# Loading x tile by tile and the value weights in four pieces in a hybrid convolution and attention kernel

## The chip, the cores and the metric

The kernel runs on one core of one Trainium2 chip, in one launch. The metric is the device time of that launch in microseconds (us); before the change its median over three runs is 1225.91 us.

## The reference

The input x has 4 images of 16 x 16 pixels with 1024 channels: 1024 tokens in all. Everything is float32. Cut to what matters:

```python
# layer 0: lambda convolution over the group-normalised x
x = x + L0_conv(_gn(x), Wq, Wk, Wv, q_*, v_*, rel_pos_emb)   # q, softmax(k), v; Yc + Yp
# layer 1: causal attention and a mixture of 8 experts
t = _to_tokens(x)
t = t + L1_attn(_ln_t(t), W_attn, b_attn, W_proj, b_proj)
t = t + L1_ffn(_ln_t(t), gate_w, gate_b, expert_w, expert_b)

def L1_attn(x, W_attn, b_attn, W_proj, b_proj):
    qkv = jnp.einsum('btc,oc->bto', x, W_attn) + b_attn
    q, k, v = jnp.split(qkv, 3, axis=2)          # 16 heads of 64
    ...                                          # masked softmax, weighted sum of v
    return jnp.einsum('btc,oc->bto', y, W_proj) + b_proj

def _ln_t(v, eps=1e-5):
    m = jnp.mean(v, axis=-1, keepdims=True)
    s = jnp.var(v, axis=-1, keepdims=True)
    return (v - m) / jnp.sqrt(s + eps)
```

The change lies where the output of layer 0 is added to x and the result is normalised for the attention (the first `_ln_t`, "layer norm 1"), and where the weights of the value projection, the last third of `W_attn`, are fetched.

## The kernel before

The kernel is one long function for one core. Layer 0 comes first (group norm, its projections, position terms), then layer norm 1 with the residual sum of layer 0, then the attention's value products, its query and key products with the softmax, the output projection, and the experts. Many products of matrices are done in Strassen's manner, with seven products of halves in place of eight, which is why sums of blocks (`sums_of_A`, L159) stand beside them.

**The stretch of the change** begins at L574. `x_at` holds all of x as eight tiles of 128 tokens (512 KB each); `xs[t]` is tile t. It takes the place of `xn`, the normalised input of layer 0, so its loads have to wait until the last product that reads `xn` (`v_product`, L538) is done. `tiles` is the order in which the tiles are worked on: the four tiles of the second halves of the images, then the four of the first halves. L578 to L580 issue all eight loads on POOL's queue, one after the other, and then the load of the bias `bp` (L589), which is 512 KB in SBUF too.

**The loop of layer norm 1** (L622 to L641) makes one pass i for each of the first seven tiles; the eighth follows behind it (L642). The order of every engine is as written here (`manual_schedule`, L621). In one pass:

- `spread(i)` (L591): `content` (L446) of the next tile, L452 on PE into PSUM and L460 on DVE, which adds it into `s0`; then the products `py` (L603) of this tile on PE, and two additions of them to `xs[t]` on DVE (L610). `s0` is filled from `two_T` by many small moves on SP's queue (L487), which were issued before.
- `layer_norm` (L192): statistics on DVE (L197 to L199), the root on ACT, and one ACTIVATE that writes the normalised rows to a slice of `ln_rows` (L170, three slices in turn; for the last two tiles L206).
- `turn_quarters(i - 2)` (L613): DVE's transpose (L187) of the tile of two passes ago into `ln1`, from its `quarters`.
- for the first six tiles, `turn_by_rows` (L210): SP writes the rows to DRAM (L212), and when they have landed reads them back in four pieces into `quarters` (`quarters_of`, L182). The last two tiles are transposed on PE instead (`turn_on_pe`, L219, with ACT's copies L223).
- in pass 3 only, L637 issues the load of `w_v[0]` on SP behind the tile's reads: the first half of the value weights, 8 blocks of 128 rows by 512 columns, as one DMA of 2 MB (`w_tile`, L123; the DMA is at L129).
- for the first six tiles, POOL adds `bp` to `xs[t]` (L638), and stores it to `x_rows` in DRAM (L639), from where the output projection takes it much later. The last two tiles are stored by SP (L641, L643).

`ln_rows`, `w_v[0]` and earlier `w_kv` come from `wpool`, a pool with two buffers: `w_v[0]` takes the buffer of `w_kv`, whose last reader is `v_product`, and `w_v[1]` (L738) takes the one of `ln_rows`.

Behind the loop, in written order too: POOL's sums of the blocks of `w_v[0]` (`sums_v`, L718), and on PE the first value products (`first`, L682, at L665) of tiles 1 and 3, the transposes of the seventh tile, the products of tile 0, the transposes of the eighth tile, and the products of tile 2. Then the load of `w_v[1]` and the other products of the first half follow. From L755 on a planner orders the instructions by its own costs until the next written order (L941): the second half of the values and the query and key products of the first pair of heads.

Of the kernel before, what the change touches and what calls it, by code (L numbers as in the profile page):

```python
# [32 lines left out]
F32 = mybir.dt.float32  # L33
# [6 lines left out]
P = 128  # L40
C = 1024
NC = C // P
# [3 lines left out]
NT = TOK // P  # L46
# [11 lines left out]
HALF = 512  # L58
# [11 lines left out]
def kernel(  # L70
# [27 lines left out]
    nc = tc.nc  # L98

    def pool(stack, name, bufs=1, **kw):  # L100
        return stack.enter_context(tc.tile_pool(name=name, bufs=bufs, reuse_waits="tile", **kw))
# [16 lines left out]
    wpool = pool(right, "wpool", 2, side="right")  # L118
# [4 lines left out]
    def w_tile(name, *parts, home=None, queue=nc.sync):  # L123

        w = (home or wpool).tile([P, NC, HALF], F32, tag="w", name=name)
        at = 0
        for part in parts:
            n = part.shape[1]
            queue.dma_start(w[:, :, at : at + n], part.rearrange("(c p) n -> p c n", p=P))  # L129
            at += n  # L130
        return w
# [60 lines left out]
    def layer_norm(ln, t, on_pe=False):  # L192


        stats = small.tile([P, 2, 6], F32, tag="ln_stats", name=f"ln1_stats{t}")
        for j in range(2):
            nc.vector.bn_stats(stats[:, j, :], xs[t][:, ts(j, HALF)])  # L197
        mv = small.tile([P, 2], F32, tag="ln_mv", name=f"ln1_mv{t}")
        nc.vector.bn_aggr(mv, stats)  # L199
        rstd = small.tile([P, 1], F32, tag="ln_rstd", name=f"ln1_rstd{t}")  # L200
        inverse_root(rstd, mv[:, 1:2], EPS)
        if on_pe:
            less = small.tile([P, 1], F32, tag="ln_less", name=f"ln1_less{t}")
            nc.vector.scalar_tensor_tensor(less, mv[:, 0:1], -1.0, rstd, ALU.mult, ALU.mult)
            for j in range(2):
                nc.scalar.activation(ln[:, ts(j, HALF)], xs[t][:, ts(j, HALF)], AF.Identity, bias=less, scale=rstd)  # L206
            return
        normalised(ln, xs[t], mv[:, 0:1], rstd)

    def turn_by_rows(ln, t, quarters, turns):  # L210
        rows = turns.tile([P, Q, C // Q], F32, tag="rows", name=f"ln1_rows{t}")
        nc.sync.dma_start(rows.rearrange("n f c -> n (f c)"), ln)  # L212
        quarters_of(rows, quarters)
# [13 lines left out]
    with ExitStack() as layer0:  # L227
# [16 lines left out]
        with ExitStack() as projection:  # L244
# [96 lines left out]
            with tc.manual_schedule():  # L341
# [6 lines left out]
                for c in range(NC):  # L348
# [10 lines left out]
                    elif NC - 4 < c < NC - 1:  # L359
                        n = c - (NC - 3)  # L360
# [26 lines left out]
            for n in (1, 2, 3, 5, 4, 7, 6):  # L387
                for pair, ((a11, a12, a21, a22), (c11, c12, c21, c22), (s1, s2, s3, s4)) in enumerate(pairs):
                    a, b = {
                        1: (a11, b11),  # L390
                        2: (a12, b21),
                        3: (s4, b22),
                        5: (s1, b11),
                        4: (a22, b21),
                        7: (s3, b12),
                        6: (s2, b22),
                    }[n]
# [28 lines left out]
            for t in range(NT):  # L426
                b, kc = divmod(t, 2)
# [147 lines left out]
        xs = [x_at[:, t, :] for t in range(NT)]  # L575
        late = pool(x_home, "late", 2, side="right")
        tiles = [(b, nt) for nt in (1, 0) for b in range(B)]
        for b, nt in tiles:  # L578
            t = 2 * b + nt
            nc.gpsimd.dma_start(xs[t], x[ts(t, P), :])  # L580

# [7 lines left out]
        def spread(i):  # L591
            b, nt = tiles[i]
            t = 2 * b + nt
            if i == 0:
                content(b, nt)
            if i + 1 < NT:
                content(*tiles[i + 1])
            for hp in range(2):
                py = mm(f"py{t}_{hp}")
                for hl in range(2):  # L600
                    bh = b * HEADS0 + 2 * hp + hl
                    for mh in range(2):
                        nc.tensor.matmul(  # L603
                            py[:, ts(hl, M)],
                            s0[:, mh, ts(nt, S2), :, bh].rearrange("p i j -> p (i j)"),
                            v_T[:, mh, ts(b, M)],
                            start=(mh == 0),
                            stop=(mh == 1),
                        )
                nc.vector.tensor_add(xs[t][:, ts(hp, HALF)], xs[t][:, ts(hp, HALF)], py)  # L610
            return t

        def turn_quarters(i):  # L613
            of, quarters = to_turn[i]
            turn(ln1[:, :, ts(of, P)], quarters)
# [2 lines left out]
            of[:, :C].rearrange("p (f c) -> p f c", f=Q)  # L618
            for of in (emb.rearrange("p c i j -> p (c i j)"), s_w.rearrange("p a c n -> p (a c n)"))
        ]  # L620
        in_order.enter_context(tc.manual_schedule())  # L621
        for i in range(NT - 1):  # L622
            t = spread(i)
            quarters = None
            if i < NT - 2:
                if i < NT - 4:
                    quarters = spare[i % 2]
                else:
                    quarters = late.tile([P, Q, C // Q], F32, tag="xg", name=f"ln1_quarters{t}")
            to_turn.append((t, quarters))  # L630
            layer_norm(ln_rows[:, i % 3, :], t, i >= NT - 2)
            if i >= 2:
                turn_quarters(i - 2)
            if i < NT - 2:
                turn_by_rows(ln_rows[:, i % 3, :], t, quarters, turns)
                if i == 3:
                    w_v = [w_tile("w_v0", W_attnT[:, 2 * C : 2 * C + HALF])]  # L637
                nc.gpsimd.tensor_add(xs[t], xs[t], bp)  # L638
                nc.gpsimd.dma_start(x_rows[ts(t, P), :], xs[t])  # L639
            else:  # L640
                nc.sync.dma_start(x_rows[ts(t, P), :], xs[t])  # L641
        t = spread(NT - 1)  # L642
# [4 lines left out]
    with ExitStack() as attention:  # L647
# [293 lines left out]
        with tc.manual_schedule():  # L941
            for d in range(len(doubles) + lag):
# [24 lines left out]
                if d < 14:  # L967
# [6 lines left out]
                    if d == 13:  # L974
                        sums.close()
                        x_pool = pool(x_home, "xb", side="right")
                        xs = [x_pool.tile([P, C], F32, tag=f"x{t}", name=f"xb{t}") for t in range(NT)]
# [120 lines left out]
    with ExitStack() as gating:  # L1098
# [350 lines left out]
        w, bias, step, T, T3, A, S = {0: w0}, {0: bias0[0]}, {}, {}, {}, {}, {}  # L1449
# [235 lines left out]
    with tc.If(count > SLOTS), ExitStack() as rest:  # L1685
        w_rest, l3 = pool(rest, "w_rest", 4), pool(rest, "l3", 3)
        for e in range(E):
            w_e = [half_weights(e, r, w_rest, "w_r") for r in range(2)]
            tiles = range(SLOTS // P, NT - 1 if e in SHORT else NT)
# [60 lines left out]
```

## Time and profile before

| what | us |
|---|---|
| median of three runs | 1225.91 |
| lowest and highest run | 1224.85 and 1229.62 |
| profiled execution, its own time | 1227.45 |
| its span (first to last instruction) | 1225.6 |
| PE busy in the span | 1208.7 |
| loads of x issued on POOL (L580) | 207.3 to 210.9 |
| additions of layer 0's output (L610) | 215.4 to 272.5 |
| load of `w_v[0]`: issue and time to landing | 252.4, 11.7 |
| first value product (L665) | 264.1 |

Times of events are counted from the start of the span. PE is the engine of the matrix products, PEld its weight loads, DVE, ACT and POOL the engines for vectors, activations and general work, and SP the engine whose queue issues most transfers. A line of the order in time has the start, the duration from first to last, the engine, the line of the kernel, the operation, what it writes and reads, the number of instructions, and in brackets how long its engine was idle before the first of them, and for whom. A line of the waits has the waiting engine and line, the one waited for, the total in us, how many times, and the longest. A line of stretches has the stretch, its length, the busy time and number of instructions of PE, PEld, DVE, ACT and POOL, the granted clock of PE, the busy share of the 16 DMA engines and the GB/s that they moved.

### The profile page before, as it was taken

How to read it: one execution, taken by the hardware profiler on the slowest of the kernel's cores; microseconds unless marked ns; L12 is line 12 of the kernel's file. 1: busy time of each engine (PE TensorE's matmuls, PEld its weight loads, DVE VectorE, ACT ScalarE, POOL GpSimd, SP SyncE). 2: the span in 40 equal slices, each digit the busy share in tenths (PEclk: the TensorE clock that was granted, in tenths of full speed). 3: DMA queues.
4: the chain of work that ended last, by engine and by line, in shares of the span. 5: the costliest groups of instructions: out<-in, count | busy, mean ns of one | idle time of the engine just before them, and what ended most of it. 6: DMA issues, size and time to landing. Idle time of an engine off the chain costs nothing.

```text
span 1225.6 us, 13283 instructions
## 1 busy us (share of the span) xinstructions
PE 1208.7 (99%) x4780; PEld 632.8 (52%) x4780; DVE 721.4 (59%) x1274; ACT 203.8 (17%) x502; POOL 401.5 (33%) x467
## 2 busy tenths in 40 slices
PE   9999999999999999999999999999999999999998
PEld 5444884778884444444444444444344334434443
DVE  5796636668332666565644567666566655565742
ACT  3310111111001222121311212101111111111110
POOL 1051351364000122222232116427443635363521
PEclk9999999999999999999999999999999999999999
DMA  9102014772201353525465646564855576556432
GB/s 349 27 1 69 18 44 123 248 251 94 69 9 60 104 172 104 170 95 181 147 213 192 206 172 238 143 185 95 246 158 141 109 230 182 144 138 180 98 82 55
DMA packets 94121, 169.77 MB, mean 139 GB/s; under 512 B 11968, under 2 KB 48848, under 8 KB 94048
## 3 DMA queue, kind: packets, MB, share of 16 engines
q1 hardware_dynamic: 73600, 108.49, 26.8%
q0 software_dynamic: 16144, 51.45, 17.3%
q10 hardware_dynamic: 4304, 8.91, 2.1%
q8 instruction: 40, 0.66, 0.2%
q14 instruction: 33, 0.27, 0.1%
HBM read 116.12 MB, written 48.50 MB: 134 GB/s over the span
## 4 chain that ended last, share of the span: by engine, by line
PE 87%; DMA 7%; DVE 3%; SPq 2%; issue 1%; ACT 1%; POOL 0%; DVEq 0%; POOLq 0%; ACTq 0%
PE p L1516 31%; PE pqk L665 15%; PE pv L665 7%; PE po L920 5%; PE pq_pair L400 4%; PE left L1558 3%; PE pq L319 3%; PE pT L510 3%; DMA ln_rows<-ln_rows 2%; PE pk L431 2%; PE sc L824 2%; PE pa L893 2%; PE rest L1572 2%; PE pv L538 2%; DMA quarters<-rows 1%; DMA s<-two_T 1%
## 5 line engine op out<-in xcount | busy, mean ns | idle before, releaser
L1041 POOL DMA_INDIRECT w_e_xg<-rows,gather x146 | 156.3, 1071 | 50.9 <-issue 41.4
L1516 PE MATMUL p<-w_e,A 128*128 128x512 f32 x368 | 163.2, 593 | 1.3 <-DVE slot L1328 1.3
L865 POOL TENSOR_TENSOR s_q<-s_q,total 128x128 f32<-128x128 f32 (+1 forms) x128 | 60.2, 506 | 276.5 <-DVE total L862 276.5
L920 PE MATMUL po<-w_p,y_T 128*128 128x512 f32 x256 | 116.8, 607 | 0.0
L1516 PEld LDWEIGHTS p<-w_e,A 128*128 128x128 f32 x368 | 69.6, 190 | 89.9 <-issue 89.0
L1064 POOL DMA_INDIRECT out_dram<-y,add x32 | 56.5, 1766 | 177.5 <-ACT y L1522 114.3
L1516 PE MATMUL p<-T,S 128*128 128x512 f32 x256 | 112.7, 593 | 0.0
L1522 ACT ACTIVATE y<-y,slot 128x512 f32<-128x512 f32 x64 | 46.2, 723 | 333.1 <-DVE y L1530 177.9
L665 PE MATMUL pqk<-ln,w_qk 128*128 128x512 f32 x192 | 85.7, 595 | 0.0
L1516 PEld LDWEIGHTS p<-T,S 128*128 128x128 f32 x256 | 48.6, 190 | 60.8 <-issue 60.5
L850 ACT ACTIVATE s_q<-sc,top 128x128 f32<-128x128 f32 (+1 forms) x128 | 52.1, 420 | 164.4 <-DVE top L846 140.6
L920 PEld LDWEIGHTS po<-w_p,y_T 128*128 128x128 f32 x256 | 47.6, 192 | 54.5 <-issue 53.5
L187 DVE STREAM_TRANSPOSE A<-w_e_xg 128x1024 f32<-128x1024 f32 x32 | 39.7, 1240 | 47.2 <-DMA w_e_xg<-rows,gather 47.2
L665 PEld LDWEIGHTS pqk<-ln,w_qk 128*128 128x128 f32 x192 | 36.1, 190 | 43.7 <-issue 41.9
L665 PE MATMUL pqk<-T,S_qk 128*128 128x512 f32 x128 | 57.8, 595 | 0.0
L1516 PE MATMUL p<-T,A 128*128 128x512 f32 x128 | 57.5, 592 | 0.0
L1516 PE MATMUL p<-w_e,S 128*128 128x512 f32 x128 | 57.5, 592 | 0.0
L665 PE MATMUL pv<-w_v,ln 128*128 128x256 f32 x192 | 43.7, 380 | 1.5 <-ACT ln L223 1.1
L319 PE MATMUL pq<-w_q,xn 128*128 128x512 f32 x96 | 44.5, 599 | 0.3 <-ACT xn L299 0.3
L1558 PE MATMUL left<-w_e,one 128*32 128x512 f32 x312 | 41.8, 593 | 0.0
L1516 PEld LDWEIGHTS p<-w_e,S 128*128 128x128 f32 x128 | 24.3, 190 | 30.6 <-issue 30.1
L1516 PEld LDWEIGHTS p<-T,A 128*128 128x128 f32 x128 | 24.3, 190 | 30.6 <-issue 30.1
(329 smaller groups left out, 1846.5 us busy)
## 6 DMA issues: line engine op xcount, KB each, us to landing
w_e<-in_expert_w_dram SPq DMA_DIRECT2D x12, 2048.0 KB, 15.2
s_rows<-s_q SPq DMA_DIRECT2D x32, 384.0 KB, 2.3
s_rows<-s_rows SPq DMA_DIRECT2D x128, 96.0 KB, 2.3
w_qk<-in_W_attnT_dram SPq DMA_DIRECT2D x8, 1024.0 KB, 5.4
w_e<-in_expert_w_dram ACTq DMA_DIRECT2D x4, 2048.0 KB, 9.5
xn<-in_xT_dram SPq DMA_DIRECT2D x8, 512.0 KB, 7.2
w_q<-in_Wq_dram SPq DMA_DIRECT2D x16, 256.0 KB, 7.3
x_at<-in_x_dram POOLq DMA_DIRECT2D x8, 512.0 KB
```

The source lines that it names most:

```text
L187: nc.vector.transpose(row_T[:, :, :slots].rearrange("p c (g j) -> p g c j", j=32), row[:, : slots // 32, :].rearrange("p g (c i) -> p g c ...
L319: nc.tensor.matmul(pq, xn[:, c, ts(t, P)], w_q[kc][:, c, :], start=(c == 0), stop=(c == NC - 1))
L400: nc.tensor.matmul(bank, a[:, c, :], b[:, c, :], start=(c == 0), stop=(c == NC // 2 - 1))
L665: nc.tensor.matmul(bank, stationary(c), moving(c), start=(c == 0), stop=(c == NC // 2 - 1))
L850: nc.scalar.activation(blocks(h, qt), psc[:, h, cols].rearrange("p (b f i) -> p b f i", f=Q, i=32), AF.Exp, bias=top[:, qt, h : h + 1], sc ...
L865: nc.gpsimd.tensor_mul(blocks(h, qt), blocks(h, qt), total[:, qt, h : h + 1].unsqueeze(2).unsqueeze(3).to_broadcast([P, 1 + qt, Q, 32]),)
L920: nc.tensor.matmul(po, y_T[:, c, ts(t, P)], w_p[j][:, c, :], start=(c == 0), stop=(c == NC - 1))
L1041: nc.gpsimd.indirect_dma_start(out=row[:, g, :], out_offset=None, in_=table[: (TOK - P) * Q, :] if e in SHORT else table, in_offset=bass.I ...
L1064: nc.gpsimd.indirect_dma_start(out=out[: TOK - P, :] if e in SHORT else out, out_offset=bass.IndirectOffsetOnAxis(ap=add[:slots, e, k : k ...
L1516: nc.tensor.matmul(bank, a[:, c, :], b[:, c, :], start=(c == 0), stop=(c == NC // 2 - 1))
L1522: nc.scalar.mul(y[i][:, ts(j, HALF)], y[i][:, ts(j, HALF)], slot[:, e, 1, 2 * pair + i : 2 * pair + i + 1])
L1558: nc.tensor.matmul(bank[ts(i, 32), :], stationary, w[of][j][:, c, :], start=(c == 0), stop=(c == NC - 1))
```

## The change

The eight loads of x are no longer issued together. A helper `load_x1(i)` issues the load of the i-th tile in the order of `tiles`; it is called for the first three tiles where all eight were, and then once in each of the passes 0 to 5, for the tile three passes ahead, on POOL's queue in front of that pass's addition of `bp`. (In pass 5 no tile is left to load.)

The tile `w_v[0]` is allocated ahead of the loop. Its load is split by rows into four DMAs of 512 KB (two blocks of 128 rows each), which are issued on SP's queue in the passes 0, 1, 2 and 3, each behind the reads of that pass's rows.

```diff
-        for b, nt in tiles:
-            t = 2 * b + nt
-            nc.gpsimd.dma_start(xs[t], x[ts(t, P), :])
+
+        def load_x1(i):
+            if i < NT:
+                b, nt = tiles[i]
+                nc.gpsimd.dma_start(xs[2 * b + nt], x[ts(2 * b + nt, P), :])
+
+        for i in range(3):
+            load_x1(i)
...
+        w_v = [wpool.tile([P, NC, HALF], F32, tag="w", name="w_v0")]
         in_order.enter_context(tc.manual_schedule())
         for i in range(NT - 1):
             t = spread(i)
...
             if i < NT - 2:
                 turn_by_rows(ln_rows[:, i % 3, :], t, quarters, turns)
-                if i == 3:
-                    w_v = [w_tile("w_v0", W_attnT[:, 2 * C : 2 * C + HALF])]
+                if i < 4:
+                    some = slice(2 * i, 2 * i + 2)
+                    nc.sync.dma_start(
+                        w_v[0][:, some, :],
+                        W_attnT[2 * i * P : (2 * i + 2) * P, 2 * C : 2 * C + HALF].rearrange("(c p) n -> p c n", p=P),
+                    )
+                load_x1(i + 3)
                 nc.gpsimd.tensor_add(xs[t], xs[t], bp)
                 nc.gpsimd.dma_start(x_rows[ts(t, P), :], xs[t])
```

## The prediction

> **What bounds the kernel now.** I read the page first, then who waited for whom on PE between 206 and 300 us (the stretch that the diff touches), then SP's queue and DVE in order of time there.
>
> ```profile
> span 1225.6 us, 13283 instructions
> ...
> PE 1208.7 (99%) x4780; PEld 632.8 (52%) x4780; DVE 721.4 (59%) x1274; ACT 203.8 (17%) x502; POOL 401.5 (33%) x467
> ```
>
> PE is idle for 1225.6 - 1208.7 = 16.9 us in the whole run. No change of loads can win more; what counts is how much of it lies here.
>
> ```profile
> PE pv L665 <- ACT ln L223: 1.1, 1, 1.1
> PE pc L452 <- DVE s L460: 0.9, 1, 0.9
> PE ln_pt L219 <- ACT ln_rows L206: 0.5, 1, 0.5
> PE pv L665 <- DMA w_v<-in_W_attnT_dram: 0.4, 1, 0.4
> ```
>
> PE's waits here are 2.9 us in all: the ceiling of a gain. Otherwise it runs one tile of layer norm 1 after another, 3.6 us of content products (L452) and 3.7 us of py (L603) overlapping a little: a period of 7.0 us (pc starts at 246.01 and 252.99).
>
> Behind the waits is SP, which takes each normalised tile i (i counts the loop's passes) through DRAM: a write (L212), a wait until it has landed, four reads (L182), then the next write.
>
> ```profile
> 225.22 2.05 SPq L487 DMA_DIRECT2D s<-two_T  x3
> 227.37 0.53 SPq L212 DMA_DIRECT2D ln_rows<-ln_rows  x1
> 232.37 1.97 SPq L182 DMA_DIRECT2D emb<-ln_rows  x4
> 234.44 0.38 SPq L212 DMA_DIRECT2D ln_rows<-ln_rows  x1
> 238.17 2.15 SPq L182 DMA_DIRECT2D s_w<-ln_rows  x4
> 240.42 0.41 SPq L212 DMA_DIRECT2D ln_rows<-ln_rows  x1
> 244.98 1.73 SPq L182 DMA_DIRECT2D emb<-ln_rows  x4
> 246.81 0.38 SPq L212 DMA_DIRECT2D ln_rows<-ln_rows  x1
> 250.42 1.87 SPq L182 DMA_DIRECT2D s_w<-ln_rows  x4
> 252.39 0.40 SPq L129 DMA_DIRECT2D w_v<-in_W_attnT_dram  x1
> 252.89 0.52 SPq L212 DMA_DIRECT2D ln_rows<-ln_rows  x1
> 265.80 2.29 SPq L182 DMA_DIRECT2D ln_quarters<-ln_rows  x4
> ```
>
> The reader is to see three things. The first write is issued at 227.37, though its tile was ready at 221.4 (ACT's L170 starts at 220.13 and takes 1.24): the moves of L487 stand in front. A cycle from write to write then takes 6.0 to 6.4 us, less than PE's 7.0, so SP catches up. And the write behind the 2 MB of w_v needs 12.9 us (252.89 to 265.80) instead of 3.6 to 4.6. DVE shows who pays:
>
> ```profile
> 237.06 1.25 DVE L187 STREAM_TRANSPOSE ln<-emb 128x1024 f32<-128x1024 f32 x1 [3.05 <-DMA emb<-ln_rows]
> 244.04 1.25 DVE L187 STREAM_TRANSPOSE ln<-s_w 128x1024 f32<-128x1024 f32 x1 [1.11 <-DMA s_w<-ln_rows]
> ...
> 270.71 1.25 DVE L187 STREAM_TRANSPOSE ln<-ln_quarters 128x1024 f32<-128x1024 f32 x1 [7.64 <-DMA ln_quarters<-ln_rows]
> ```
>
> The late first turn costs DVE 3.05 us and PE 0.91 at 238.93 (some 2.1 us of DVE delay are absorbed by banks). The turn behind w_v holds the last tile's L610 until 271.88, and with it the ACT steps for which PE waits 0.54 and 1.06 us.
>
> **x loads.** All eight stay on POOL, 0.53 us of issue each. Three go out at 207; x3, in pass 0, stands before the first L638, so right behind bp; x4 to x7 follow in passes 1 to 4, each behind the x_rows store of the pass before: about 224.7, 231.7, 238.6 and 246. They are first read by L610 at 246.38, 252.26, 258.49 and 271.88 now, so even 2.5 us earlier each has over 12 us to land. POOL idles 3.0 to 5.8 us ahead of each L638, which waits for ACT: the moved issues cost nothing. Without that idle time it would be 0.53 us per pass, on a chain that ends in the x_rows store only.
>
> What is gained: between 207 and 224 the loads fill the DMA.
>
> ```profile
> DMA packets 2403, 5.16 MB, mean 304 GB/s; under 512 B 433, under 2 KB 1379, under 8 KB 2403
> ...
> SPq L487 <- DMA s<-two_T: 4.7, 7, 1.1
> ```
>
> 2 of 4.2 MB leave this stretch. The second line, of SP's waits from 204 to 228, is what SP lost to slow landings; I take half as saved, 2.3 us (bounds 0 and 4.7, since the first four tiles still collide). SP's first write moves from 227.4 to about 225.
>
> **Weight pieces.** One DMA of 2 MB becomes four of 512 KB, each behind the reads of passes 0 to 3; three more issues are 3 x 0.39 = 1.2 us on SP, spread over four cycles. A piece stands in SP's queue ahead of the next pass's write, which the next reads wait for, for which DVE waits two passes later, and PE behind DVE. So its price is a longer cycle. The trace has 2 MB in front of one write: 12.9 - 3.6 = 9.3 us, 2.3 per piece, but with two x_rows stores beside it, and start-up. An x tile's 128 packets of 4 KB took about 160 ns on one of 16 engines, 1.3 us in all; I take 1.4 for a piece (bounds 1.3 and 2.3). The x tile that now comes beside it is another 1.3 us of DMA time, on POOL's queue: the stores there lengthen cycles by 0 to 0.4, so I take 0.3 (bounds 0 and 1.3). The cycle becomes 6.2 + 1.4 + 0.3 = 7.9 us (bounds 7.5 and 9.8) for passes 1 to 4, against PE's 7.0. Whole-stretch traffic allows it:
>
> ```profile
> 227.40:252.40 25.00, 24.09 (x87) 18.29 (x86) 17.59 (x36) 5.29 (x7) 9.82 (x7) 1.00 0.64 219
> 252.40:264.40 12.00, 11.58 (x45) 9.42 (x45) 8.69 (x19) 2.89 (x5) 4.76 (x4) 1.00 0.96 323
> ```
>
> DMA is busy for 0.64 (last column but one) of the 25 us; four tiles and four pieces add 4 x 1.3 + 4 x 1.4 = 10.8 us to 16.0: 26.8 over some 30 us, nearly full. That is the weak point of the change.
>
> [...] no one waits for a single piece; in the trace eight loads of 512 KB leave POOL within 4.2 us and move back to back. I take the trace's value[...].
>
> **The sum.** First write 225; the second a cycle of 6.7 later, 231.7 (piece 0 comes behind the reads, so it delays only the write after); write n then at 231.7 + 7.9 (n-1), n = 4 at 255.4. Quarters are turned about 2.2 us after the next write's issue: turns 0 to 3 can go at 233.9, 241.8, 249.7, 257.6. DVE reaches them at 234.0, 241.0, 248.4 and 256.3; lateness of 0.8 to 1.3 us per pass, a third of it reaching PE. What follows turn 3 in DVE is turn 1.25 and L460 1.25, then PE's last py 3.7, in sum (with a handover of 0.1) 6.3: the first pv starts at 263.9 (now 264.08). No wait for w_v: piece 3, issued near 255, lands by 260. Turn 4 can go at 265.5, five us earlier than 270.71, so the last tile is normalised while PE does its 32 pv (7.0) and 8 transposes (1.04), 16 pv (3.7), 8 transposes (1.36) and a rest of 0.3 for L223's copy: 13.4. The pv that starts at 278.75 now starts at 263.9 + 13.4 = 277.3: **1.45 us won**. All behind it shifts along: w_v1's load is released by the same transposes, POOL's sums of w_v by the last py. The profiled execution took 1227.45 for its span of 1225.6; minus 1.5 this is 1226.0. It lies 1.5 above the median 1225.91, 0.1%; so the forecast is 1225.9 - 1.5 = **1224.4 us**.
>
> **Rivals.**
>
> *SP keeps up* (cycle near 7, first write at 223 to 224): turn 3 is ready before DVE, PE only loses the 0.3: 2.9 - 0.3 = 2.6 us, 1223.3. For it: 2.7 us in each cycle are pure latency, in which POOL's transfers fit. Against: the pieces share SP's own queue.
>
> *SP becomes the bound* (slower). The point is the cycle: the pv starts at turn 3 + 19.7, turn 3 = 233.9 + 3 cycles, so 278.75 is reached at 8.4 us, and every us beyond costs 3. At 9.4 it is +3 us, 1229; only from 10.4, +6 us, would it be slower measurably. For it: the 2.3 us per piece measured, [...]the nearly full DMA. Against: 1.3 us per 512 KB of packets.
>
> *It changes nothing that lasts*: behind L755 a planner orders the remaining value and first query/key products; another start may give another order there, and the 1.5 us are regained or lost: 1224 to 1228.
>
> **How the numbers follow.** About 0.5% (6 us) is what a measurement of this kernel can tell from no change. My forecast 0.40, SP keeps up 0.25, SP the bound 0.22 (0.07 of it beyond +6 us), planner 0.13. A gain over 6 us would need twice the idle time of this stretch: 0.03, for the planner or the spread of runs (1224.85 to 1229.62). Faster 0.03, same 0.90, slower 0.07. The range takes in the full 2.6 us and 2 us of spread below, SP's cycle of 9.4 and some spread above: 1221.0 to 1230.0.
>
> **What would show it.** SP's first L212 near 225; L212 to L212 near 7.9 in passes 1 to 4 (over 8.4 refutes the gain); no PE wait on w_v; L187's 7.64 gone, replaced by waits near 1 us in passes 3 to 5; PE's waits from 206 to 280 at about 1.5 instead of 2.9. If PE's waits there pass 9 us, the forecast is wrong, and the piece or the x tile was mispriced.

## The result: slower, and the profile after

| what | before | after |
|---|---|---|
| median of five runs each, us | 1224.85 | 1235.29 |
| ratio, 95% interval | | 1.0067 [1.005, 1.0084] |
| profiled execution and its span, us | 1227.45, 1225.6 | 1235.35, 1233.5 |
| first value product (L665, now L676), us | 264.08 | 276.01 |

One of the five executions after ran in a slow state (1583.89 us), so the ratio is that of the other four: the change costs 0.67%, some 8 us. The lines of the changed kernel that answer to those shown of before follow; lines behind L580 have moved down by 5 to 11. First, for whom PE waited from 206 to 290 us (total, times, longest):

```profile
PE pc L452 <- DVE s L460: 8.0, 2, 4.2
PE pv L676 <- ACT ln L223: 0.2, 1, 0.2
```

Of the four old waits two are gone and that for ACT's copy is 0.2 us, but the one for L460 has grown from 0.9 to 8.0 us. SP's queue in order of time:

```profile
225.03 0.80 SPq L212 DMA_DIRECT2D ln_rows<-ln_rows  x1
231.26 1.97 SPq L182 DMA_DIRECT2D emb<-ln_rows  x4
233.32 0.40 SPq L644 DMA_DIRECT2D w_v<-in_W_attnT_dram  x1
233.82 0.41 SPq L212 DMA_DIRECT2D ln_rows<-ln_rows  x1
242.13 2.04 SPq L182 DMA_DIRECT2D s_w<-ln_rows  x4
244.22 0.43 SPq L644 DMA_DIRECT2D w_v<-in_W_attnT_dram  x1
244.75 0.41 SPq L212 DMA_DIRECT2D ln_rows<-ln_rows  x1
250.84 1.90 SPq L182 DMA_DIRECT2D emb<-ln_rows  x4
252.78 0.43 SPq L644 DMA_DIRECT2D w_v<-in_W_attnT_dram  x1
253.32 0.41 SPq L212 DMA_DIRECT2D ln_rows<-ln_rows  x1
263.04 1.86 SPq L182 DMA_DIRECT2D s_w<-ln_rows  x4
264.94 0.43 SPq L644 DMA_DIRECT2D w_v<-in_W_attnT_dram  x1
265.47 0.41 SPq L212 DMA_DIRECT2D ln_rows<-ln_rows  x1
```

The first write goes out at 225.03, but from write to write it is now 8.8, 10.9, 8.6 and 12.2 us, against PE's 7.0 per tile. A write needs 6.1 to 9.7 us until the reads behind it can be issued; before it was 3.6 to 5.0, but for the one write behind the 2 MB of weights. SP has become the bound of the loop. DVE's turns pay for it, and PE behind DVE:

```profile
239.86 1.25 DVE L187 STREAM_TRANSPOSE ln<-emb 128x1024 f32<-128x1024 f32 x1 [6.30 <-DMA w_v<-in_W_attnT_dram]
248.03 1.25 DVE L187 STREAM_TRANSPOSE ln<-s_w 128x1024 f32<-128x1024 f32 x1 [2.30 <-DMA s_w<-ln_rows]
260.82 1.25 DVE L187 STREAM_TRANSPOSE ln<-emb 128x1024 f32<-128x1024 f32 x1 [5.91 <-DMA emb<-ln_rows]
```

(The turn does not read `w_v`; a wait is put down to what landed last.) And something that the traces of before do not show in this stretch: PE in order of time, and stretches with PE's granted clock (last column but two):

```profile
233.85 3.71 PE L608 MATMUL py<-v_T,s 128*128 128x256 f32 x16
241.73 6.64 PE L452 MATMUL pc<-q,k_q 128*128 128x512 f32 x8 [4.17 <-DVE s L460]
...
262.69 6.41 PE L452 MATMUL pc<-q,k_q 128*128 128x512 f32 x8 [3.79 <-DVE s L460]
```

```profile
241.70:248.40 6.70, 6.67 (x9) 2.99 (x10) 4.02 (x10) 1.44 (x2) 1.27 (x1) 0.55 0.98 297
248.40:258.90 10.50, 10.50 (x40) 8.36 (x39) 5.21 (x11) 1.44 (x2) 4.56 (x4) 1.00 0.85 207
```

Towards the end of each of the two gaps, at 240.87 and 261.35 us, the granted clock of this trace falls to half, for 6.83 us each time, and the eight content products take 6.64 and 6.41 us instead of 3.60.

What PE did up to the first value product, added up: waits 8.0 instead of 0.9 + 0.4, so +6.7; half clock 3.04 + 2.81 = +5.9; the stretch begins 0.45 us earlier (the first pc at 206.09, not 206.54). Sum +12.1; measured 276.01 - 264.08 = +11.9. This adds up what happened, not what caused it: the time lost in the first slow stretch would otherwise have gone into the next wait for DVE. Behind the first value product 2.2 us come back, 1.4 of them from the two waits for ACT, so the products of tile 2 start at 288.52 instead of 278.75, 9.8 us later. Most of the way from there to the 7.9 us between the spans lies elsewhere: the profiled execution of before ran at half clock for 3.4 us near 704 us as well (the 256 products of the output projection took 116.8 us, after 115.1, so 1.7 us were lost), and that of after did not.

### The profile page after: what moved, and what is told of

Its sections match the earlier page's. It is cut to its first block, busy times and chain, and to the rows that moved or that the text cites. A ratio compares the mean times of both kernels' runs of the same rounds, so it can differ in the third digit from the quotient of the medians.

```text
span 1233.5 us, 13287 instructions
## 1 busy us (share of the span) xinstructions
PE 1211.3 (98%) x4780; PEld 633.3 (51%) x4780; DVE 721.2 (58%) x1274; ACT 203.6 (17%) x502; POOL 403.4 (33%) x467
## 3 DMA queue, kind: packets, MB, share of 16 engines
q10 hardware_dynamic: 4304, 8.91, 2.1%
## 4 chain that ended last, share of the span: by engine, by line
PE 87%; DMA 6%; SPq 3%; DVE 3%; issue 1%; ACT 0%; POOL 0%; DVEq 0%; ACTq 0%; POOLq 0%
PE p L1527 31%; PE pqk L676 15%; PE pv L676 8%; PE po L931 5%; PE pq_pair L400 4%; PE left L1569 3%; PE pq L319 3%; PE pk L431 2%; SPq L487 2%; PE sc L835 2%; PE pa L904 2%; PE rest L1583 2%; PE pv L538 2%; PE pT L510 2%; DMA quarters<-rows 2%; DMA ln_rows<-ln_rows 1%
## 5 line engine op out<-in xcount | busy, mean ns | idle before, releaser
L931 PE MATMUL po<-w_p,y_T 128*128 128x512 f32 x256 | 115.1, 599 | 0.0
L676 PE MATMUL pqk<-ln,w_qk 128*128 128x512 f32 x192 | 85.7, 595 | 0.0
L676 PEld LDWEIGHTS pqk<-ln,w_qk 128*128 128x128 f32 x192 | 36.1, 190 | 43.7 <-issue 42.3
L676 PE MATMUL pqk<-T,S_qk 128*128 128x512 f32 x128 | 57.8, 595 | 0.0
L676 PE MATMUL pv<-w_v,ln 128*128 128x256 f32 x192 | 43.5, 380 | 0.2 <-ACT ln L223 0.2
L452 PE MATMUL pc<-q,k_q 128*128 128x512 f32 x64 | 34.5, 692 | 8.0 <-DVE s L460 8.0
L891 DVE STREAM_TRANSPOSE s_T<-s_rows 128x768 f32<-128x768 f32 x32 | 30.3, 964 | 20.3 <-DMA s_rows<-s_rows 20.3
```

The source lines that it names most:

```text
L676: nc.tensor.matmul(bank, stationary(c), moving(c), start=(c == 0), stop=(c == NC // 2 - 1))
L931: nc.tensor.matmul(po, y_T[:, c, ts(t, P)], w_p[j][:, c, :], start=(c == 0), stop=(c == NC - 1))
```

## The experiments

Three causes were to be told apart: the x tiles (X), the weight pieces in SP's queue (W), and the half clock (C). Each ratio is to the kernel before on the chip of that run; not all runs had the same chip. Cuts in the diffs are marked `...`.

**One half of the change at a time.** `e1_x_only` keeps the x loads of the change and takes the weights back to one load in pass 3:

```diff
-                if i < 4:
-                    ...
+                if i == 3:
+                    w_v = [w_tile("w_v0", W_attnT[:, 2 * C : 2 * C + HALF])]
                 load_x1(i + 3)
```

> The x half of the change alone: three tiles of x at once and the others three passes ahead, with the value weights in one DMA of 2 MB in pass 3 as in the kernel before. Theory X (the x tiles, with the x_rows stores on the same queue, stand packet by packet among SP's reads): the reads of pass 0 land some 6 us after their issue instead of 2.6, DVE waits 5 us or more for turn 0, PE waits 3 us or more for L460 there, and the time is 3 to 6 us above the kernel before. Theory W (the weight pieces in SP's queue ahead of the writes decide): the first write goes out at 225, cycles stay at 6.2 to 6.6 us, PE waits for L460 under 1 us, and the time is 1 us below to 0.5 us above the kernel before.

Measured: 1.0036 [1.0019, 1.0054]; PE waits 3.5 us for L460 once, with 3.4 us of half clock behind it (the mean clock from 225 to 270 us is 0.96, before 1.00). SP, then DVE and PE:

```profile
231.61 2.07 SPq L182 DMA_DIRECT2D emb<-ln_rows  x4
233.79 0.38 SPq L212 DMA_DIRECT2D ln_rows<-ln_rows  x1
240.74 1.73 SPq L182 DMA_DIRECT2D s_w<-ln_rows  x4
```

```profile
239.76 1.25 DVE L187 STREAM_TRANSPOSE ln<-emb 128x1024 f32<-128x1024 f32 x1 [5.63 <-DMA emb<-ln_rows]
```

```profile
241.63 5.40 PE L452 MATMUL pc<-q,k_q 128*128 128x512 f32 x8 [3.50 <-DVE s L460]
```

No weight is under way here, and yet the last read of pass 0, issued at 233.2, lands at 239.6: 6.3 us instead of 3.0. Where that time goes shows in the DMA queues from 234.5 to 236.5 us, in the middle of those reads (q0 is POOL's queue, q1 SP's; packets, MB, share of the 16 engines):

```profile
q0 software_dynamic: 89, 0.36, 78.5%
q1 hardware_dynamic: 22, 0.02, 5.0%
```

In the same two us of the trace of before SP's queue has 90.5%, and POOL's moves nothing. Theory X holds as first put: an x tile beside a pass is not hidden. Not all of the loss in this trace is the wait: 3.4 us of half clock also fall on the value products of tile 2, of which more in the last section.

`e2_w_only` loads all eight tiles at once again and keeps the four pieces:

```diff
-        for i in range(3):
+        for i in range(NT):
             load_x1(i)
...
-                load_x1(i + 3)
```

> The weight half of the change alone: all eight tiles of x at once as before, the value weights in four pieces behind the reads of passes 0 to 3. Theory W: writes 1 to 4 take 6 to 8 us to land behind their piece, PE waits near 8 us for L460, and the time is 6 to 9 us above the kernel before. Theory X: a piece costs the 1.4 us of its packets, cycles are near 7.6 us from a first write at 227.4, PE waits under 3 us, and the time is within 2 us of the kernel before.

Measured: 1.005 [1.0032, 1.0068]. SP:

```profile
233.40 0.40 SPq L644 DMA_DIRECT2D w_v<-in_W_attnT_dram  x1
233.89 0.41 SPq L212 DMA_DIRECT2D ln_rows<-ln_rows  x1
240.02 1.94 SPq L182 DMA_DIRECT2D s_w<-ln_rows  x4
```

Writes 1 to 4 take 6.1, 6.1, 6.6 and 6.7 us behind their piece, where 3.6 to 4.6 were needed before; cycles are 8.6 to 9.1 us. So a piece costs 2 to 3 us, not the 1.4 of its packets. That is theory W for the cycles, but PE's waits for L460 are 2.7 + 1.9 = 4.6 us, half of what it expected (with 3.4 us of half clock behind the longest, 2.4 us). Both halves hurt. Their losses add up to 1.0086; together they measured 1.0067, and with intervals of 0.0017 on each side the difference is not shown.

**The half clock.** `e3_warm` fills PE's two gaps with products that nobody reads:

```diff
+            if i in (3, 5):
+                warm = ps.tile([P, 2, HALF], F32, tag="sc", name=f"warm{i}", bufs=1)
+                for _ in range(5):
+                    nc.tensor.matmul(warm[:, 0, :], ident, v_T[:, 0, :HALF], start=True, stop=True)
             if i + 1 < NT:
                 content(*tiles[i + 1])
```

> The changed kernel, with five products of 128x512 that nobody reads put on PE ahead of the content products of passes 3 and 5 (some 4.3 us each), where PE now stands idle for 4.17 and 3.79 us. Loads and waits are those of the changed kernel. Theory C (a part of the loss is not the waiting but PE running at half its clock for 6.8 us after each of the two gaps): the granted clock stays at full in the loop, the content products behind the gaps take 3.6 us instead of 6.4 to 6.6, and the time is 4 to 6 us below the changed kernel. If only the waiting costs, the time is that of the changed kernel within 1 us.

Measured: 1.0065 [1.0042, 1.0088], not to be told from the changed kernel. The five products took 4.46 us each time, the clock stayed at full (0.999 over the span), each group of content products took 3.6 to 3.7 us, and the first value product came at 272.16, 3.9 us earlier in the profiled execution; but SP's writes 1 to 5 went out at 234.6, 245.5, 253.5, 263.8 and 273.5, within 1.7 us of the changed kernel's. SP still set the pace of the loop, and the unread products filled the time for which PE stands idle in the changed kernel. The expectation of 4 to 6 us failed; the intervals are too wide to exclude a gain of 2 or 3 us, and the run does not price the clock by itself.

**The queue of the pieces.** `e4_act` issues them from ACT:

```diff
-                    nc.sync.dma_start(
+                    nc.scalar.dma_start(
                         w_v[0][:, some, :],
```

> The changed kernel, with the four weight pieces issued on ACT's queue instead of SP's, at the same places; the x tiles as in the change. Theory W in its narrow form (a piece delays the write because it stands ahead of it in one queue): writes land after 4 to 6 us again, cycles are 6.5 to 7.5 us, and the time is within 2 us of the kernel before. If the price is that of the shared DMA engines, the reads and writes are slowed by the pieces all the same, cycles stay above 8 us, PE still waits 4 us or more, and the time stays 4 us or more above the kernel before.

Measured: 1.0055 [1.0033, 1.0077]. From pass 2 on the writes land after 4.1, 5.1 and 3.6 us again and cycles are 5.9 to 7.4, as the narrow form of W has it. But the first two, beside pieces and x tiles, took 7.7 and 8.1 us, PE waited once for 6.0 us, and half clock followed (content products of 5.89 us instead of 3.60). So the other queue takes the piece out of the write's way from pass 2 on, and the first two passes are slow all the same. The x tiles are still in this kernel, and its time can be told neither from e1's nor from the changed kernel's.

**Weights placed behind a write, not ahead of one.** `e5_w_late` is the kernel before, with the 2 MB load moved: `between` issues it in pass 4, and it no longer stands in pass 3. (Where this line was added, the lines behind it stand one lower.)

```diff
         nc.sync.dma_start(rows.rearrange("n f c -> n (f c)"), ln)
+        between()
         quarters_of(rows, quarters)
```

> The kernel before, with one thing moved: the 2 MB load of the value weights is issued in pass 4 between SP's write and its reads, instead of in pass 3 ahead of that write. Theory W (what stands in SP's queue ahead of a write delays the whole cycle): the write of pass 4 lands after some 4 us instead of 12.9, the reads land behind the weights near 265 instead of 270.7, DVE's wait of 7.6 us for that turn shrinks to some 2 us, PE's waits of 0.5 and 1.1 us for ACT go, and the time is 1 to 2 us below the kernel before. If place in the queue is of no account (the DMA engines are simply full), the turn comes at 270 as before and the time is unchanged.

Measured: 1.0026 [1.0014, 1.0038], slower where 1 to 2 us less were expected. The write landed after 4.1 us as expected, but the reads, now behind 2 MB, landed at 269.5, and the weights at 267.4, 3.4 us later than before: the first of the 16 parts landed at 262.5, the last at 267.4. PE waited 4.2 us for them and then ran at half clock (32 value products in 9.61 us, before in 7.17):

```profile
267.43 9.61 PE L666 MATMUL pv<-w_v,ln 128*128 128x256 f32 x32 [4.23 <-DMA w_v<-in_W_attnT_dram]
```

Behind this gap PE waits for only 0.2 us more up to the products of tile 2, so `e9_w_late_warm` puts the clock's question again there, with 15 small products on `ident` (3.51 us in the trace) ahead of the first value product:

```diff
+        warm = ps.tile([P, 2, HALF], F32, tag="sc", name="warm", bufs=1)
+        for _ in range(15):
+            nc.tensor.matmul(warm[:, 0, :P], ident, ident, start=True, stop=True)
         seconds = [first(0, 1, tr, tr), first(0, 3, mm, tr)]
```

> The kernel with the weights' load behind the write of pass 4, where PE stood idle for 4.2 us ahead of the first value product and then ran at half its clock for 6.8 us, with 15 products of 128x128 that nobody reads put in front of that value product (some 4.1 us at full clock). The weights still land near 267. Theory C (the half clock is a cost of its own behind a gap): the clock stays at full, the 32 value products take 7.1 us instead of 9.6, and the time is 2 to 3 us below that kernel's, at or under 1.001 of the kernel before. If the slow stretch costs nothing beyond the wait, the ratio stays at 1.0026.

```profile
266.95 7.17 PE L666 MATMUL pv<-w_v,ln 128*128 128x256 f32 x32 [0.36 <-DMA w_v<-in_W_attnT_dram]
```

The same 32 products took 7.17 us instead of 9.61, and the products of tile 2 began at 279.56 instead of 282.48: the half clock cost some 2.4 us in these traces. In time: 1.0018 [1.001, 1.0027] against 1.0026 [1.0014, 1.0038]; the medians differ by 2.3 us, but the two ran on different chips, the intervals overlap, and the time expected was missed.

**Why an x tile costs so much.** In the changed kernel the 4 KB packets of POOL's queue between 224 and 256 us take 217 ns on average (up to 2.5 us), before 167 ns. `e6_x_ahead` is e1 with each load ahead of its pass's store, not right behind one, and the first four tiles loaded at once. (The changed kernel and e1 do that in effect: nothing stands on POOL between the third load and the one of pass 0.)

```diff
-        for i in range(3):
+        for i in range(4):
             load_x1(i)
...
-                load_x1(i + 3)
                 nc.gpsimd.tensor_add(xs[t], xs[t], bp)
+                load_x1(i + 4)
                 nc.gpsimd.dma_start(x_rows[ts(t, P), :], xs[t])
```

> The x half alone once more (weights in one DMA in pass 3), with the order on POOL's queue turned around: in passes 0 to 3 the load of the tile four passes ahead goes out before the x_rows store of the pass, not right behind it; the first four tiles are loaded at once, as they are in effect in the changed kernel. Theory S (it is the load directly behind a store in one queue whose packets become slow, 0.3 to 2.5 us each instead of 0.16): packets of x stay under 0.25 us, the reads of pass 0 land 3 us after issue, PE waits under 1 us for L460, and the time comes within 1 us of the kernel before. Theory X as first put (the added bytes stand among the reads, whatever their order): the reads of pass 0 still land 5 us or more after issue, and the time is 3 to 5 us above.

Measured: 1.0029 [1.0015, 1.0043], PE waits 3.2 us once with 6.8 us of half clock (content products of 6.74 us); the last read of pass 0 landed 6.9 us after its issue. The packets still take 227 ns on average, and the reads are as late as in e1. Theory S falls: the order within the queue is not it.

`e7_x_act` issues the last four tiles from ACT, 2.8 to 6.8 us ahead of their times in e1:

```diff
-                load_x1(i + 3)
+                load_x1(i + 4, nc.scalar)
```

> The x half alone, with the loads of the last four tiles issued on ACT's queue, in passes 0 to 3 right behind the normalising ACTIVATE, some 2.8 us ahead of the pass's x_rows store; the first four tiles at once on POOL. Theory S: with store and load in two queues the packets stay fast; reads land after 3 us, and the time is within 1 us of the kernel before. Theory X: the same bytes at about the same time cost the same; reads of pass 0 or the write beside them take 2 to 3 us longer, and the time is 2 to 5 us above.

Measured: 1.0017 [1.0006, 1.0028], some half of e1's loss, though the intervals overlap; PE waits 1.8 us once, and the clock stays at full there (content products of 3.70 us). The tile of pass 1 moves beside SP's write (issued at 226.6, landed at 231.6), not beside the reads. Whether the other queue or the earlier time helps was not separated.

**The pieces in SP's gap.** `e8_w_gap` loads all eight tiles at once and issues each piece between a pass's write and its reads, in the time in which SP waits; `between` is the issue of a piece in passes 0 to 3:

```diff
         nc.sync.dma_start(rows.rearrange("n f c -> n (f c)"), ln)
+        between()
         quarters_of(rows, quarters)
```

> The weight half alone (all eight tiles of x at once), with each of the four pieces issued between SP's write and its reads of passes 0 to 3, instead of behind the reads. Theory W: the 1.4 us of a piece now move in the 2 to 3 us in which SP waits for the write to land; writes land after 3.7 to 4.5 us again, cycles are 6.2 to 6.8 us, PE's waits in the stretch fall below 1.5 us, and the time is 1 to 2.5 us below the kernel before. If a piece costs its time wherever it stands, cycles stay near 8.7 us as with the pieces behind the reads, and the time is 4 to 6 us above.

Measured: 0.999 [0.9981, 1.0]: the 0.5% loss of e2 is gone, and only the place of the four DMAs has changed. SP:

```profile
239.90 0.59 SPq L212 DMA_DIRECT2D ln_rows<-ln_rows  x1
240.53 0.43 SPq L645 DMA_DIRECT2D w_v<-in_W_attnT_dram  x1
244.26 1.74 SPq L182 DMA_DIRECT2D emb<-ln_rows  x4
246.09 0.38 SPq L212 DMA_DIRECT2D ln_rows<-ln_rows  x1
```

Writes take 3.3 to 4.6 us again (one 6.0), cycles after the second are 5.9 to 6.6, PE waits for L460 (here L461) for 1.2 us in the stretch, and the first value product is at 263.08. The pieces now stand ahead of the reads, and those of passes 0 and 3 do land later, 5.3 and 4.2 us after their issue where it was 3.1 and 2.9. But SP waits only for the landing of its write; behind the reads it issues the next write at once, and DVE needs them two passes later. The time expected, 1 to 2.5 us less, lies inside the interval; a gain is not shown.

`e10_gap_x` adds the x loads of the change to e8:

```diff
-        for i in range(NT):
+        for i in range(3):
             load_x1(i)
...
+                load_x1(i + 3)
                 nc.gpsimd.tensor_add(xs[t], xs[t], bp)
```

> The changed kernel, x tiles and all, with the one thing moved that the runs point to: each weight piece is issued between SP's write and its reads instead of behind the reads. Theory of two separate prices (pieces ahead of a write cost 2 us a cycle, x tiles beside the reads of pass 0 cost 3 to 4 us there): the x part's price is left, PE waits 3 to 4 us for L460 once and runs at half clock behind it, and the time is 3 to 5 us above the kernel before. If only the sum of both is too much for the DMA engines, the time is within 1 us of the kernel before.

Measured: 1.0027 [1.0018, 1.0036], against 1.0067 [1.005, 1.0084] for the change, from which it differs only in the place of the pieces. The x part's price is back:

```profile
242.30 6.41 PE L453 MATMUL pc<-q,k_q 128*128 128x512 f32 x8 [4.70 <-DVE s L461]
```

The two prices are separate, as the first of the two expectations had it.

**The last wait.** `e12_gap_turn` is e8 with tile 0's turn moved one pass on:

```diff
             t = spread(i)
+            if i == 3:
+                turn_quarters(0)
...
-            if i >= 2:
+            if i >= 3:
                 turn_quarters(i - 2)
```

> All eight tiles of x at once, pieces between write and reads, and the first turn moved: DVE transposes tile 0 in pass 3, behind the additions of that pass, instead of at the end of pass 2, where it is the last wait left (3.4 us on DVE, 1.2 us on PE). Expected: PE's wait of 1.2 us for L460 goes, no other takes its place (pass 3 has 1.25 us more on DVE, within what the banks absorb), and the time is 2 to 3 us below the kernel before, 1 us below the kernel with the pieces alone. If DVE's longer pass 3 is what PE then waits for, the time is that of the kernel with the pieces alone.

Measured: 1.0059 [1.0041, 1.0077]. Tile 2's reads go into tile 0's buffer and now stand ahead of its turn, so tile 0's place is filled from tile 2's rows and tile 0 is left out. DVE waited for them for 11.2 us and PE for 10.2, with 10.2 us of half clock (the mean clock from 225 to 270 us is 0.89). `e13_gap_turn` gives tile 2 another buffer:

```diff
-                if i < NT - 4:
+                if i < NT - 4 and i != 2:
                     quarters = spare[i % 2]
```

> All eight tiles of x at once, weight pieces between SP's write and reads, the first turn moved from the end of pass 2 to pass 3 behind that pass's additions, and now tile 2's rows read into a buffer of their own (in e12_gap_turn they overwrote tile 0's before its turn, which changed the result's part of that tile and made the turn wait for them). Expected: no PE wait over 0.5 us in the stretch, first value product near 262, time 2 to 3 us below the kernel before (ratio 0.9975 to 0.9985). If DVE's longer pass 3 takes the place of the wait, PE still waits about 1 us and the ratio is that of e8_w_gap, 0.999.

Measured: 0.9981 [0.9973, 0.9989], median 1222.48 us against 1224.74: the fastest kernel here, and 0.2% faster than before. The ratio is the one expected, but by luck: its way is another. DVE's wait for turn 0 is gone, but it waits 2.1 us for turn 1 instead, and PE still waits 1.1 us, as in e8:

```profile
246.37 3.70 PE L453 MATMUL pc<-q,k_q 128*128 128x512 f32 x8 [1.12 <-DVE s L461]
```

The intervals of e8 and e13 overlap, so nothing shows that the moved turn adds anything to the moved pieces.

## Why the prediction was wrong

The likeliest case, 1.45 us won, failed. What came is the second rival, "SP becomes the bound", which had 0.22, and 0.07 for a loss of the size measured. The chain, SP's cycle, then DVE's turn, then PE, was read rightly. The step that failed is the size of SP's cycle, 6.2 + 1.4 + 0.3 = 7.9 us: both prices in it were too low. In the passes 1 to 3 the cycle was 6.15 us on average before, 7.93 with the x tiles alone (e1) and 8.91 with the pieces alone (e2). So an x tile adds 1.8 us and a piece 2.8, both above the bounds given, 1.3 and 2.3. The sum, 6.15 + 1.8 + 2.8 = 10.7, fits the 10.55 measured with both. Step by step:

- *First write near 225*: right, 225.03.
- *No wait on w_v, and the waits at the last tile gone*: right; 0.2 us was left, for which 0.3 had been taken.
- *A piece costs 1.4 us of cycle*: mis-sized by half. The 2.3 per piece measured in the trace of before was at hand as the upper bound, and the price was taken from packet times instead, because nobody waits for a piece. But the write behind it is waited for: it takes 6.1 to 6.7 us behind a piece (e2), and 3.3 to 4.6, once 6.0, ahead of one (e8). What makes up the 1.4 us beyond the packets was not separated.
- *An x tile costs 0.3 us of cycle (bounds 0 and 1.3)*: mis-sized by a factor of six. The last read of pass 0 lands 3.3 us later, while POOL's queue holds most of the DMA engines. The row used, stores on POOL's queue that lengthened cycles by 0 to 0.4, is that of one transfer per pass and gives no price for a second one.
- *Piece 0 delays only the write after*: right for the piece, but the first cycle was 8.8, not 6.7. Without any piece, in e1, it is 8.7: it is the x tile of pass 1, issued at 224.2, beside the first write. (The first cycle before was 7.1 us, above the 6.0 to 6.4 that the prediction read.)
- *Cycle 7.9*: it was 10.9, 8.6 and 12.2 in passes 1 to 3. With the writes as measured, the prediction's own sum nearly comes out: write 4 at 265.47, and 2.2 and 19.7 us to the products of tile 2, is 287.4; they came at 288.52. Its sign for a lost gain, a cycle over 8.4, showed; PE's waits, 8.2 us, stayed below the 9 that it named as well.
- *The clock*: no case had it. Its price is smaller than the 5.9 us of slow products: by the prediction's sum turn 3, at 268.08, allows the first value product 6.3 us later, at 274.4, and it came at 276.01. That is an estimate of 1.6 us, and no run measured it in the changed kernel. The two gaps here were 4.17 and 3.79 us; a wait of 2.4 us in e2 was followed by half clock too (last section).
- The DMA engines were expected to be "nearly full", and were busy for 0.86 of the time from 225 to 270 us. That alone is not the price: e10 moves the same tiles and pieces in that time, at a share of 0.90, and loses less than half as much.

## What to carry to other kernels

When a queue carries a round trip, ask for which landing the queue itself waits before it goes on. Place a prefetch behind the write that is waited for, not ahead of it: the same four DMAs of 512 KB cost 0.5% in one place and nothing in the other. The gap has a size: behind 2 MB in such a gap (e5) the reads landed 12.0 us after their issue, not 3. When a loop turns data through DRAM in step with the matrix engine, ask for the time from write to write against the engine's time per tile, and take off loads that were done early at no cost only if that leaves room.

## What the runs showed of the hardware

In the traces of these runs, PE's granted clock fell to half at some of PE's waits. Waits of 1.8 and 1.9 us in the loop (e7, e2) came with none: the products behind the one of e7 took 3.70 us, and e2's mean clock from 225 to 270 us, 0.96, leaves room for little more than the one stretch at its longer wait. Waits of 2.4 and 3.5 us came with 3.4 us at half (e2, e1; content products of 5.40 us), 3.2 to 6.0 us with 6.8 us (e6, both gaps of the change, e5, e10, e4; content products of 5.89 to 6.74 us, in e5 the value products of 9.61), and 10.2 us with 10.2 (e12; 5.89 us). The stretches measured are thus one, two or three times 3.4 us, and waits of like length came with one or two. In e1 the two old waits for ACT, of 0.5 and 1.1 us with 1.4 us of transposes between them, came with 3.4 us at half as well:

```profile
281.30 1.36 PE L219 MATMUL ln_pt<-ident,ln_rows 128*128 128x128 f32 x8 [0.53 <-ACT ln_rows L206]
283.72 5.36 PE L671 MATMUL pv<-w_v,ln 128*128 128x256 f32 x16 [1.05 <-ACT ln L223]
```

The products took 5.36 us where before, behind the same two waits, they took 3.72 at full clock. What decides between the two is not settled by these runs. Near 704 us it is the same: the profiled executions of before, e9 and e13 have a stretch at half there, and those of after and e8 do not (mean clock of the whole span 0.997, 0.997 and 0.998; e8 0.999; that of after, 0.993, holds its two long stretches), for a wait there of 1.4 to 2.4 us in each (before and e9 1.9, e13 2.4; after 1.4, e8 2.4). The 1.7 us lost there before suggest that as much of the spread between executions of one kernel can come from this alone: an estimate from the traces of before and after.

The 16 parts of one DMA of 2 MB ended from 262.5 to 267.4 us in e5, 4.9 us apart, and from 261.7 to 264.0 before, 2.3 us apart.
